# A convolution block followed by a selective scan: another order of work at the scan's first and last units

## The chip, the cores and the metric

The kernel runs on one core of one Trainium2 chip. A core has five engines that run side by side, each through its own list of instructions in order: TensorE (PE), VectorE (DVE), ScalarE (ACT), GpSimd (POOL) and SyncE (SP), which here only issues DMAs. They hand work to each other through semaphores. The metric is the device time of one execution in microseconds (us); the median of three runs of the kernel before is 3618.1 us (3617.41 to 3619.6).

## The reference

Two layers over a batch of 32 images of 96 channels, 56 x 56 pixels, all float32. The first is a ConvNeXt block. The second is a 5x5 depthwise convolution with SiLU, whose result `xs` (32 x 96 x 3136 tokens) goes into a selective scan with N = 4 states per channel. Only the scan is touched by the change:

```
x_dbl = einsum('kd,bdl->bkl', x_proj_w, xs)
dts, Bs, Cs = x_dbl[:, :R], x_dbl[:, R:R+N], x_dbl[:, R+N:]
delta = softplus(einsum('dr,brl->bdl', dt_w, dts) + dt_b)
log_dA = maximum(delta[:, :, None, :] * A, LOG_EPS)
P = exp(cumsum(log_dA, axis=-1))
dB_u = delta[:, :, None, :] * Bs[:, None] * xs[:, :, None]
hs = P * cumsum(dB_u / maximum(P, EPS), axis=-1)
y = einsum('bdnl,bnl->bdl', hs, Cs) + xs * Ds
```

## The kernel before

There are four stages, one after another: the 7x7 convolution, the MLP with its normalisation, the 5x5 convolution, and the scan (from line 587). The first three leave `xs` in DRAM as `conv2_d` (the profile calls it `conv_d`), one row of 32 x 56 values per channel and image row.

The scan works in *steps*. A step `k` is one half (1568 tokens) of one image; 64 steps in all, and two images together make a *piece* of two steps, which is loaded by `load(p)` as one tile `xs_p` of 96 partitions. Each step is cut into three *units* of 32 channels by 4 states, which fill 128 partitions; 192 units. A half step (784 tokens) is numbered `h`.

Per step, in the order in which the data flow:

- `delta_in(k, h)` (L635): matmuls give the input of Softplus in PSUM (`pz`).
- `delta(k, h)` (L643): ACT's Softplus writes it into `du[:, 0]`.
- `delta_x(k, h)` (L649): POOL multiplies it by `xs` into `du[:, 1]`.
- `keep_du(k, h)` (L654): SP stores both to DRAM (`du_d`).
- `rows_bc(k)`, `rows_out(k)` and `spread(k, kind, h)` (L657 to L687): PE and ACT make B (`bt`, kind 0) and C (`ct`, kind 1) on 128 partitions.

Per unit:

- `spread_du(i)` (L689): SP reads `du_d` back with every channel repeated four times, into `rep_i` (two halves of 1568: delta, and delta times x). Five buffers.
- `decay(i)` (L698): three ACT passes over the delta half of `rep_i`; the first is Exp.
- `drive(i)` (L705): POOL multiplies the other half by `bt`.
- `scan(i)` (L709): DVE runs a product scan (L717), a combination with the driven half (L720) and the scan proper (L724), into `hs_i`. The running product lies in PSUM (`pv`).
- `weigh(i)` (L729): POOL saves the last column of the state if another half follows, then multiplies `hs_i` by `ct`.

Per step, at the end: `gather(k, h)` (L737) sums over states and adds `xs * Ds` by matmul into PSUM (`py`), `store(k, h)` (L755) copies it on ACT and ACT issues the DMA to `out`.

The order is written out by hand in the loop at L769 and held by `pin`, which keeps the program's order on each engine. A pass `i` handles unit `i` at its scan; what comes before it is done in passes ahead (`spread_du` four ahead, `decay` two, `drive` one), `weigh` one pass later, `gather` and `store` three or more later. The piece `p` of pass `i` is `(i + 8) // 6`, with `at` the place in it. The first piece is loaded in pass -11; its four Softplus halves are in pass -8, its stores in passes -6 to -3 with the load of the second piece (pass -5) among them, and the first `spread_du` in pass -4. The second piece's Softplus is in pass -2, and `decay(1)` comes after it, in pass -1. All PSUM tiles of the scan but `pv` rotate through two buffers of two banks (`bank_pair`). ACT changes its function table between Softplus and Exp.

## Time and profile before

| What | Value |
|---|---|
| median of three runs | 3618.1 us |
| the profiled execution | 3618.94 us, span 3617.1 us |
| DVE busy / PE / ACT / POOL, share of the span | 74% / 84% / 65% / 55% |
| last store of the 5x5 convolution issued | 1815.13 us |
| first piece's load issued, first matmul on it | 1819.02 us, 1827.04 us |
| first instruction of the first scan (L717) | 1859.70 us |
| first instruction of the second unit's scan | 1875.80 us |
| end of the last unit's scan (L724 at 3599.21 for 3.48) | 3602.69 us |
| end of the span | 3617.1 us |

The profile is one execution; its times count from the start of the span. It has a page with busy shares, the chain that ended last and the costliest groups of instructions. A timeline lists instructions in order of time; a line gives start, duration, engine, line of code, operation, what is written and read, and in brackets how long the engine had been idle and what ended that. "SPq" and "ACTq" are the issues of DMAs, without the transfer itself.

### The profile page before, as it was taken

What the parts mean: (1) busy time and instruction counts of PE and PEld (TensorE: products, weight loads), DVE (VectorE), ACT (ScalarE), POOL (GpSimd) and SP (SyncE); (2) the same over time, 40 slices, a digit from 0 to 9 for tenths busy, and PEclk for the clock granted to TensorE, in tenths of its full rate; (3) what the DMA queues carried; (4) which work ended last, traced back from release to release, by engine and by line L of the source; (5) the groups of instructions that cost most, each with busy time, mean ns of one, the idle gap of its engine ahead of it and who ended that gap; (6) DMA issues with size and microseconds to landing.
All of it is one profiled execution on the core that took longest, in us unless ns stands there. A gap on an engine that the chain in (4) does not pass through costs nothing. (4 is left out here: it accounts for less than half of the span.)

```text
span 3617.1 us, 46656 instructions
## 1 busy us (share of the span) xinstructions
PE 3051.3 (84%) x17290; PEld 1285.1 (36%) x17290; DVE 2659.5 (74%) x1816; ACT 2347.6 (65%) x2166; POOL 1973.9 (55%) x1286
## 2 busy tenths in 40 slices
PE   8999998999999999899848777777777778777775
PEld 5777775333333333333312222222222222222221
DVE  6666666333333333799949999999999999999998
ACT  4555554333333333588758888887888887888884
POOL 2333343222222222000048899998999998999996
PEclk9999999999999999999956667666667666767666
DMA  6655555444444542799977877877877877877873
GB/s 184 194 179 167 172 171 168 157 158 159 157 160 158 158 157 81 220 283 286 276 237 247 279 257 262 286 260 257 282 255 261 288 257 252 287 250 268 286 255 110
DMA packets 307052, 793.92 MB, mean 219 GB/s; under 512 B 124089, under 2 KB 185553, under 8 KB 282153
## 3 DMA queue, kind: packets, MB, share of 16 engines
q1 hardware_dynamic: 260176, 671.66, 57.6%
q0 software_dynamic: 29632, 80.27, 7.1%
q10 hardware_dynamic: 17016, 39.01, 2.9%
q8 instruction: 137, 2.24, 0.3%
q14 instruction: 91, 0.74, 0.1%
HBM read 555.05 MB, written 235.74 MB: 219 GB/s over the span
## 5 line engine op out<-in xcount | busy, mean ns | idle before, releaser
L735 POOL TENSOR_TENSOR hs<-hs,ct 128x1568 f32<-128x1568 f32 x192 | 672.9, 3504 | 106.1 <-DVE hs L724 96.8
L717 DVE TENSOR_TENSOR_SCAN pv<-rep,pv 128x1568 f32<-128x1568 f32 x192 | 664.5, 3461 | 73.3 <-ACT rep L703 56.0
L707 POOL TENSOR_TENSOR rep<-rep,bt 128x1568 f32<-128x1568 f32 x192 | 674.4, 3513 | 15.3 <-DMA rep<-du_d 15.3
L431 ACT ACTIVATE g<-ph,b1p_t 128x896 f32<-128x896 f32 x336 | 320.4, 1005 | 511.6 <-PE ph L421 511.5
L451 DVE SCALAR_TENSOR_TENSOR o<-po,b2r_t,x 128x224 f32<-128x224 f32 x336 | 190.6, 608 | 568.1 <-PE po L440 568.1
L334 PE MATMUL ps<-xq,wt 120*112 120x448 f32 x1536 | 582.9, 540 | 20.2 <-DMA wt<-taps_d 17.9
L463 POOL DMA_DIRECT2D block_d<-o x336 | 183.1, 552 | 659.2 <-DVE o L451 625.2
L334 PEld LDWEIGHTS ps<-xq,wt 120*112 120x112 f32 x1536 | 428.7, 280 | 172.7 <-issue 20.2
L421 PE MATMUL ph<-h,w1r_t 32*128 32x448 f32 x4032 | 438.2, 558 | 24.7 <-DVE h L411 22.6
L652 POOL TENSOR_TENSOR du<-du,xs 96x784 f32<-96x784 f32 x128 | 236.1, 1846 | 372.4 <-ACT du L646 372.4
L638 PE MATMUL pz<-xs,wd_t 96*96 96x392 f32 x512 | 276.5, 705 | 173.2 <-ACT du L646 137.6
L440 PE MATMUL po<-g,w_t 128*32 128x448 f32 x4032 | 413.0, 543 | 0.0
L748 PE MATMUL py<-hs,sel_t 128*32 128x392 f32 x1536 | 328.2, 684 | 72.2 <-POOL hs L735 72.2
L683 PE MATMUL pk<-bn,pick_t 8*128 8x392 f32 x1024 | 288.9, 684 | 100.2 <-ACT y L758 81.2
L720 DVE SCALAR_TENSOR_TENSOR pv<-pv,rep 128x1568 f32<-128x1568 f32 x192 | 345.6, 1800 | 21.1 <-POOL hs L735 1.4
L533 PE MATMUL ps<-xq,wt 128*32 128x448 f32 x3072 | 308.7, 547 | 41.8 <-DMA xq<-block_d 39.8
L724 DVE TENSOR_TENSOR_SCAN hs<-rep,carry_h,pv 128x1568 f32<-128x1568 f32 x96 | 334.0, 3480 | 10.8 <-PE pk L683 0.5
L556 DVE COPY st<-yt 28x896 f32<-28x896 f32 x288 | 317.2, 1101 | 33.0 <-ACT yt L547 14.4
L724 DVE TENSOR_TENSOR_SCAN hs<-rep,pv 128x1568 f32<-128x1568 f32 x96 | 328.4, 3421 | 9.9 <-DVE pv L720 0.5
L701 ACT ACTIVATE rep<-rep,a_t 128x1568 f32<-128x1568 f32 x192 | 308.4, 1606 | 13.5 <-DMA rep<-du_d 13.1
L702 ACT ACTIVATE rep<-rep,lift_t 128x1568 f32<-128x1568 f32 x192 | 307.7, 1602 | 6.2
L703 ACT ACTIVATE rep<-rep,lift_t 128x1568 f32<-128x1568 f32 x192 | 307.6, 1602 | 6.3
(84 smaller groups left out, 3188.3 us busy)
## 6 DMA issues: line engine op xcount, KB each, us to landing
rep<-du_d SPq DMA_DIRECT2D x192, 1568.0 KB
du_d<-du SPq DMA_DIRECT2D x128, 588.0 KB
xq<-block_d SPq DMA_DIRECT2D x192, 225.0 KB
block_d<-o POOLq DMA_DIRECT2D x336, 120.0 KB, 5.8
xt<-in_x_dram SPq DMA_DIRECT2D x192, 196.0 KB
x<-in_x_dram SPq DMA_DIRECT2D x336, 112.0 KB
h<-conv_d SPq DMA_DIRECT2D x84, 448.0 KB
conv_d<-st SPq DMA_DIRECT2D x96, 392.0 KB
```

Source lines behind the costliest of these rows:

```text
L334: nc.tensor.matmul(ps[:, j].rearrange("p (i r) -> p i r", i=BI), lhsT=wv[:KR, t], rhs=xq[:KR, j, :, t : t + W2], start=(t == 0), stop=(t = ...
L421: pin(nc.tensor.matmul(phs[i // 2][:, i % 2, :HALF], lhsT=w1r_t[rows, d, f * 128 : (f + 1) * 128], rhs=hts[n, d][rows, s * HALF : (s + 1) ...
L431: nc.scalar.activation(gt, ph[:, :, :HALF], AF.Gelu, bias=b1p_t[:, f : f + 1], scale=1.0)
L440: pin(nc.tensor.matmul(po[CB * i : CB * i + CB, :HALF], lhsT=w2_t[:, f, CB * d : CB * d + CB], rhs=gts[n, s, f, i // 2][:, i % 2], start=( ...
L533: pin(nc.tensor.matmul(ps[RW * f : RW * f + RW, h, : B * QW].rearrange("p (b q) -> p b q", q=QW), lhsT=wv[:, f, t], rhs=xv[:, :, t : t + Q ...
L556: pin(copy(st[:, :, :, :, f], yt[RW * f : RW * f + QR].rearrange("p h (b q) -> p h b q", q=QW),))
L707: pin(nc.gpsimd.tensor_mul(ut, ut, bts[i // NG]))
L717: pin(nc.vector.tensor_tensor_scan(grown, da, zero, pv[:, last : last + 1] if q else 1.0 / EPS, ALU.mult, ALU.add))
L720: pin(nc.vector.scalar_tensor_tensor(run, in0=grown, scalar=1.0, in1=ut, op0=ALU.min, op1=ALU.mult))
L724: pin(nc.vector.tensor_tensor_scan(ht, da, run, carry_h[:, col : col + 1] if q else 0.0, ALU.mult, ALU.add))
L735: pin(nc.gpsimd.tensor_mul(ht, ht, cts[k]))
L748: pin(nc.tensor.matmul(py[g * DG : (g + 1) * DG, s, :BK], lhsT=sel_t, rhs=hss[k * NG + g][:, cols], start=False, stop=True, tile_position= ...
```

## The change

It touches the first passes and the last of the scan's loop; the passes between keep their order.

At the front, all of the first piece's work is written out in pass -8. The first load is cut into one DMA per image. A one-column Softplus (`warm`) is put ahead of everything. For the first image, delta alone is stored and read back (`spread_du(0, deltas)`), and delta times x, on DVE, follows with a store and a read of its own. Units 1 and 2 are read next, then the second piece is loaded, then `decay(0)`, `drive(0)`, and the second image's delta, on POOL as before. In pass -2 `decay` and `drive` of units 1 and 2 stand ahead of the second piece's Softplus. At the end, the last `weigh` is cut in two (DVE and POOL), the last step's `gather` takes units 0 and 1 in the pass before unit 2's, and the last `store` is copied by DVE and issued by SP.

```diff
         def load(p):
...
-            pin(nc.sync.dma_start(
-                xt, conv2_d[:, q * HQ : (q + 1) * HQ, b * W : (b + NI) * W]
-            ))
+            rows = conv2_d[:, q * HQ : (q + 1) * HQ, b * W : (b + NI) * W]
+            for i in range(1 if p else NI):
+                cols = slice(None) if p else slice(i * W, (i + 1) * W)
+                pin(nc.sync.dma_start(xt[:, :, cols], rows[:, :, cols]))
...
-        def delta_x(k, h):
+        def delta_x(k, h, engine=nc.gpsimd):
...
-            pin(nc.gpsimd.tensor_mul(u, d, tokens(k, h, 2)))
+            pin(engine.tensor_mul(u, d, tokens(k, h, 2)))
...
-        def keep_du(k, h):
-            pin(nc.sync.dma_start(du_d[k][:, :, h * HT : (h + 1) * HT], dus.pop((k, h))))
+        def keep_du(k, h, part=slice(0, 2)):
+            pin(nc.sync.dma_start(
+                du_d[k][:, part, h * HT : (h + 1) * HT], dus[k, h][:, part]
+            ))
...
-        def spread_du(i):
+        def spread_du(i, part=slice(0, 2)):
...
+            to = reps[i][:, part].rearrange("p i t -> p (i t)")
+            du = du_d[k, g * DG : (g + 1) * DG, part, :]
+            src = bass.AP(du.tensor, du.offset, [du.ap[0], [0, N], [1, to.shape[1]]])
+            pin(nc.sync.dma_start(to, src))
...
-            pin(nc.gpsimd.tensor_mul(ht, ht, cts[k]))
+            if i < units - 1:
+                pin(nc.gpsimd.tensor_mul(ht, ht, cts[k]))
+            else:
+                for engine, cols in (nc.vector, slice(0, HT)), (nc.gpsimd, slice(HT, CH)):
+                    pin(engine.tensor_mul(ht[:, cols], ht[:, cols], cts[k][:, cols]))
...
-        def gather(k, h):
+        def gather(k, h, parts=range(NG)):
...
-        def store(k, h):
+        def store(k, h, copy=nc.scalar.copy, queue=nc.scalar):
...
+            if p == 0 and at == 0:
+                deltas, products = slice(0, 1), slice(1, 2)
+                warm = pool.tile([C, 1], F32, name="warm", bufs=1)
+                pin(nc.scalar.activation(warm, dtb_t, AF.Softplus))
+                for h in range(2):
+                    delta_in(0, h)
+                for h in range(2):
+                    delta(0, h)
+                for h in range(2):
+                    keep_du(0, h, deltas)
+                spread_du(0, deltas)
+                for h in range(2):
+                    delta_x(0, h, nc.vector)
+                    keep_du(0, h, products)
+                rows_bc(0)
+                rows_out(0)
+                spread_du(0, products)
+                for u in range(1, NG):
+                    spread_du(u)
+                load(1)
+                for h in range(2):
+                    spread(0, 0, h)
+                decay(0)
+                drive(0)
+                for h in range(2):
+                    delta_in(1, h)
+                    delta(1, h)
+                    delta_x(1, h)
+                    keep_du(1, h)
+                continue
...
+            ready = {-2: [1, 2], -1: [], 0: []}.get(i, [i + 2])
+            driven = {-2: [1, 2], -1: [], 0: [], 1: []}.get(i, [i + 1])
...
-            at_unit(i + 2, decay)
-            at_unit(i + 1, drive)
+            for u in ready:
+                if u:
+                    at_unit(u, decay)
+            for u in driven:
+                if u:
+                    at_unit(u, drive)
...
-            if g == 0 and 0 <= after < steps:
+            if g == 0 and 0 <= after < steps - 1:
                 gather(after, 0)
                 store(after, 0)
                 gather(after, 1)
+            if i == units - 1:
+                for h in range(2):
+                    gather(steps - 1, h, range(NG - 1))
+            if i == units:
+                for h in range(2):
+                    gather(steps - 1, h, range(NG - 1, NG))
+                store(steps - 1, 0)
+                store(steps - 1, 1, nc.vector.tensor_copy, nc.sync)
```

## The prediction

> **What bounds the kernel now.** I read the page first, then the timelines of DVE, ACT, POOL and SP from 1795 to 1960 us, then the last 80 us. Between its two ends the scan is DVE's: from the second unit at 1875.80 to 3602.69 it runs 191 units, 9.04 us each, and its three rows alone give 3.461 + 1.800 + about 3.45 = 8.71.
>
> ```profile
> L717 DVE TENSOR_TENSOR_SCAN pv<-rep,pv 128x1568 f32<-128x1568 f32 x192 | 664.5, 3461 | 73.3 <-ACT rep L703 56.0
> L720 DVE SCALAR_TENSOR_TENSOR pv<-pv,rep 128x1568 f32<-128x1568 f32 x192 | 345.6, 1800 | 21.1 <-POOL hs L735 1.4
> ```
>
> Of the 73.3 us that DVE stood idle before L717, 44.63 + 7.31 are the start and 1.15 follows at unit 7. So the time is: when DVE gets going, plus the units, plus the 14.4 us after DVE's last scan. The change works on the first and the last term. DVE's start:
>
> ```profile
> 1859.70 3.43 DVE L717 TENSOR_TENSOR_SCAN pv<-rep,pv 128x1568 f32<-128x1568 f32 x1 [44.63 <-ACT rep L703]
> 1875.80 3.43 DVE L717 TENSOR_TENSOR_SCAN pv<-rep,pv 128x1568 f32<-128x1568 f32 x1 [7.31 <-ACT rep L703]
> 1893.57 3.43 DVE L717 TENSOR_TENSOR_SCAN pv<-rep,pv 128x1568 f32<-128x1568 f32 x1
> 1930.41 3.49 DVE L717 TENSOR_TENSOR_SCAN pv<-rep,pv 128x1568 f32<-128x1568 f32 x1 [1.15 <-ACT rep L703]
> ```
>
> These are units 0, 1, 3 and 7. What they waited for stands on SP's queue:
>
> ```profile
> 1819.02 0.31 SPq L621 DMA_DIRECT2D xs<-conv_d  x1
> 1834.17 0.65 SPq L655 DMA_DIRECT2D du_d<-du  x1
> 1834.86 0.61 SPq L621 DMA_DIRECT2D xs<-conv_d  x1
> 1835.99 5.43 SPq L655 DMA_DIRECT2D du_d<-du  x1
> 1846.95 0.55 SPq L695 DMA_DIRECT2D rep<-du_d  x1
> ```
>
> The second store of the first image stands behind the second piece's load, and the read of unit 0 waits 5.5 us more for it. Unit 1 was in place by 1863.77 (POOL drives it then), but its decay starts at 1870.90, because ACT does the second piece's Softplus from 1859.68 to 1869. The end:
>
> ```profile
> 3602.84 3.48 POOL L735 TENSOR_TENSOR hs<-hs,ct 128x1568 f32<-128x1568 f32 x1 [5.59 <-DVE hs L724]
> 3606.37 2.82 PE L748 MATMUL py<-hs,sel_t 128*32 128x392 f32 x8 [7.56 <-POOL hs L735]
> 3609.13 2.02 PE L741 MATMUL py<-xs,dsm_t 96*96 96x392 f32 x4
> 3611.07 1.52 PE L748 MATMUL py<-hs,sel_t 128*32 128x392 f32 x12
> 3612.64 0.81 ACT L758 COPY y<-py 96x784 f32<-96x784 f32 x1 [2.60 <-PE py L748]
> 3613.48 0.32 ACTq L759 DMA_DIRECT2D out_dram<-y  x1
> ```
>
> The transfer takes from 3613.48 to the end at 3617.1, 3.6 us for 294 KB.
>
> **What the Trainium skill says.** "ScalarE: Activation LUTs", What ACT_TABLE_LOAD costs, gives about 1.28 us for a change of table; the trace has 1.28 at 1830.01, after the wait for PE. "DMA: Bandwidth & Descriptors", Why small descriptors are slow, gives three cycles on top of one per 32 bytes: 17 for 448 bytes, 10 for 224; no row here shows 224. "SBUF — State Buffer", Who interferes with whom, says that a DVE instruction with two SBUF inputs and a GpSimd one that reads SBUF exclude each other; the scan's DVE rows have one operand in PSUM, so the trace doesn't test it. "TensorE: Matmul & The Clock Gate", Part 1, says that the clock doubles after some 3.4 us of work; here matmuls on `pz` take 0.65 us from 1827.04 and 0.33 from about 1832.3.
>
> **The front, step by step.**
> *Load.* The first piece took 8.0 us from issue to matmul, about 5.2 of them transfer (DMA is busy from 1821 to about 1826). Half of it in as many pieces of half the size takes between 2.6 and 5.2 us; by the skill's 10/17 it is 3.1. I take 1.6 us earlier, 1825.4, with 0 and 2.6 as ends. I assume that the matmul waits for its own image alone: ACT wrote its column of the last `st` (1809.05) before DVE wrote the interleaved others (1812.22), so interleaved parts are told apart.
> *Delta.* The first Softplus comes 2.97 us after the data, as before, without the table load (`warm` does it while ACT waits, 19.20 us idle). The second half's matmuls end 5.3 us after the data; 0.91 for Softplus: 1831.9.
> *Store and read delta.* The store is as large as the final output's, 3.6 us: 1835.5. The read of a full unit took 7.85 us (1846.95 to Exp at 1854.80); half the bytes at 430 GB/s (windows 1855 to 1870) save 1.9, and no store shares the queue: 5.2, so 1840.7. Decay is three passes of 1.64: 1845.6, first scan instruction, 14 us earlier than before.
> *Products.* DVE's multiplication, about 0.95 from 1.083 for 128x896 in the normalisation, lies under the wait for the store. Its two stores are issued after the read of delta, for SP waits at that read; with 1.9 us of read and 2.5 of store (602 KB at 236 GB/s, window 1837 to 1841) ahead they land at about 1843. Read 5.2, `drive` 3.5: L720 at 1851.7, unit 0 ends at 1857.1.
> *Units 1 and 2, second piece.* From 1843 the queue holds 0.8 + 1.6 + 1.6 MB of reads, 9.3 us at 430 GB/s, then the second piece, 5.2. With 1.9 to start and 1.2 to finish, unit 1 is there at 1851.7, unit 2 at 1855.5, the second piece at 1860.6; before it was there at 1845.57. Decays end at 1857.2 and 1862.1 and scans run 1857.3 to 1866.2 and 1866.2 to 1875.1. Image 1's products on POOL stand behind `drive(0)` and end at 1855.4; their stores follow the load, about 1867, and unit 3's read is there by 1873.
> *The new wait.* In pass -2 PE's matmuls on the second piece wait for it to 1860.6, and behind them on PE stand `ct` of step 0, `rows_bc(1)` and `bt` of step 1; behind these on ACT stands `decay(3)`. From the load: 3.0 to the first Softplus; with two banks, the four are done after 11.9 if PE stays at 0.65, after 9.3 if it speeds up; two copies of `ct` 2.1, `pn` and its copy 2.9, `bt` 3.8, table 1.3, decay 4.9, which makes 26.9 or 23.5 with the faster matmuls counted throughout. Unit 3 can scan at 1884.1 to 1887.5, against 1893.57: 6 to 9.5 earlier, though DVE stands idle for 9 to 12 us before it.
> *What is late next.* POOL can weigh unit 0 only with `ct`, 11 to 14 us after the load. Three weighs, one `drive`, two products (3 x 3.5 + 3.5 + 2 x 1.85) bring `weigh(2)` to 1889.6 to 1892.4, against 1897.46. It releases `gather`, the two copies at 1900.38 and 1906.07, after which ACT runs `bt`, `decay(6)`, Softplus and `decay(7)` without slack: the wait of 1.15 at unit 7. So what arrives at unit 7 is 5.1 to 7.9. I take 6.5. Beyond it the order is the old one, and before only 2.9 us of idle time before L717 remain to the end.
>
> **The end.** After 3602.69 DVE weighs half a tile (0.95), POOL the other (1.75). The gather of units 0 and 1 and of `xs` is done by then, hidden beside unit 191's scan. What remains are eight matmul records of one column group, which can't run beside each other (four of a group take 1.52 us fast, 2.8 slow): 5.4 slow, about 4.3 if the clock rises midway, as it did at 3610. From 3603.8 to 3608.1 or 3609.2; DVE's copy from PSUM is about 0.97 (0.55 for 384 columns in `w1r_t`), the output 3.6: 3612.7 to 3613.8, so 3.3 to 4.4 less. If DVE and POOL exclude each other, 0.9 to 1.7 of it is lost. I take 3.8.
>
> **Sum.** 6.5 + 3.8 = 10.3 us off the profiled execution's 3618.94, or 3608.6; the median of runs lies 0.8 lower: 3608.
>
> **Rivals.**
> *Everything is hidden.* Should ACT reach `decay(3)` by 1875 after all, DVE runs on from unit 2: 18.5 + 3.8, 3596. For it: DVE's own units leave no more. Against it: PE's and ACT's order put eight dependent exchanges behind the second piece. Chance 0.10.
> *The gain at the front is given back.* The second piece comes 6.5 us later than I have it, or the first image's matmul waits for both halves in pieces that cost as much as whole ones (5.2 + 1.6 later): then the change doesn't do what it says at the front, and the end alone remains, 3614. For it: the load has been put behind 4 MB of reads, and the queue did hold SP up (5.43 us for one issue). Against it: 430 GB/s while such reads ran. Chance 0.20.
> *The second piece becomes the bound.* If the reads of units 0 to 2 ran at 215 GB/s (window 1875 to 1880 has that) and the load with them at half speed, the load would land about 14 us later; PE, and ACT and POOL behind it, stand still. From 10.3 us late on the whole is a loss, from 17.5 on over 0.2%; at 19 late, 3627. Against it: little else moves then. Chance 0.08.
>
> **How the numbers follow.** The forecast has 0.62, with 3603 to 3611 as its own range. A measurement of this kernel can tell about 0.2%, 7.2 us, from no change: below 3610.9 is faster, above 3625.3 slower. Faster: nearly all of the forecast and the first rival, 0.70. Within 0.2%: the second, a little of the forecast and of the third, 0.22. Slower 0.08. The range, 3601 to 3616, leaves out most of the first and third rivals.
>
> **What would show it.** First L717 near 1846, L720 of unit 0 some 2.5 us after the first scan's end; `pz` of the second piece starting near 1860; DVE idle for 9 to 12 us before unit 3, released by ACT L703; unit 7 at about 1924. At the end, 10 to 11 us after the last scan instead of 14.4. It would be wrong if unit 3 starts later than 1891, or if the middle's 9.04 us per unit changes.

## The result, and the profile after

| What | Before | After |
|---|---|---|
| median of the timed runs | 3618.42 us (3612.85 to 3621.63, 6 runs) | 3598.3 us (3597.0 to 3600.45, 6 runs) |
| ratio to before, 95% interval | | 0.9946 [0.9933, 0.9959] |
| the profiled execution, its span | 3618.94 us, 3617.1 us | 3600.45 us, 3598.7 us |

The changed kernel is faster by 20.1 us by the medians and by 18.4 us between the two spans, where 10.3 had been forecast. The kernel after ran again in two later sets, beside the kernel before on the same chip: 3596.47 us against 3614.91 (18.4 less) and 3598.98 against 3615.83 (16.9 less).

An absolute time of the trace holds everything that came before it. The first piece's load is issued at 1819.02 us in the trace before and at 1817.32 in the one after. The program up to there is the same, and over all traces of this study the issue lies between 1809.96 and 1819.02 without relation to any edit. So from here on the landmarks count **from the issue of the first piece's load**:

| From the issue of the first load, us | Before | After | Change |
|---|---|---|---|
| first matmul on the first piece | 8.02 | 5.32 | -2.70 |
| first scan, unit 0 | 40.68 | 24.78 | -15.90 |
| first matmul on the second piece | 26.55 | 39.82 | +13.27 |
| scan of unit 3 | 74.55 | 61.95 | -12.60 |
| scan of unit 7 | 111.39 | 98.51 | -12.88 |
| end of the last scan | 1783.67 | 1771.09 | -12.58 |
| from there to the end of the span | 14.41 | 10.29 | -4.12 |

So, between these two traces, 12.6 come from the front and 4.1 from the end, and 1.7 of the difference of the spans lie before the change begins. From unit 7 to the last scan's end it is 1672.3 before and 1672.6 after: the middle is as it was, as far as single traces tell, which differ by up to 6 us there (see below). From the load's issue to the end of the span the kernel after, traced three times, is 16.7 to 18.1 us shorter than the one trace of before.

The two rows of the costliest groups that answer to those shown of before (columns: line, engine, operation, operands, count | busy, mean ns of one | idle time before):

```profile
L721 DVE TENSOR_TENSOR_SCAN pv<-rep,pv 128x1568 f32<-128x1568 f32 x192 | 664.5, 3461 | 42.8 <-ACT rep L707 24.9
L724 DVE SCALAR_TENSOR_TENSOR pv<-pv,rep 128x1568 f32<-128x1568 f32 x192 | 345.6, 1800 | 22.6 <-POOL rep L711 1.6
```

Read alone, the first row tells too much: 73.3 - 42.8 is 30.5 us less idle time. But DVE now has work earlier, and part of its idle time stands before that. From DVE's timeline of the kernel after, the two products and the first rows of units 0, 1, 3 and 7:

```profile
1826.52 0.97 DVE L653 TENSOR_TENSOR du<-du,xs 96x784 f32<-96x784 f32 x1 [12.94 <-ACT du L647]
1828.88 0.97 DVE L653 TENSOR_TENSOR du<-du,xs 96x784 f32<-96x784 f32 x1 [1.40 <-ACT du L647]
1842.10 3.43 DVE L721 TENSOR_TENSOR_SCAN pv<-rep,pv 128x1568 f32<-128x1568 f32 x1 [12.24 <-ACT rep L707]
1847.15 1.80 DVE L724 SCALAR_TENSOR_TENSOR pv<-pv,rep 128x1568 f32<-128x1568 f32 x1 [1.63 <-POOL rep L711]
...
1852.50 3.43 DVE L721 TENSOR_TENSOR_SCAN pv<-rep,pv 128x1568 f32<-128x1568 f32 x1
...
1879.27 3.43 DVE L721 TENSOR_TENSOR_SCAN pv<-rep,pv 128x1568 f32<-128x1568 f32 x1 [9.10 <-ACT rep L707]
...
1915.83 3.49 DVE L721 TENSOR_TENSOR_SCAN pv<-rep,pv 128x1568 f32<-128x1568 f32 x1 [0.87 <-ACT rep L707]
```

The products take 12.94 + 0.97 + 1.40 + 0.97 = 16.3 us out of the first scan's idle time, and L724 has 1.5 more; 30.5 - 16.3 - 1.5 = 12.7, which is the front's gain. Unit 1 follows unit 0 without a pause (7.31 before), and the new pause of 9.10 stands at unit 3. SP's queue in the kernel after:

```profile
1817.32 2.30 SPq L624 DMA_DIRECT2D xs<-conv_d  x2
1826.51 2.68 SPq L656 DMA_DIRECT2D du_d<-du  x2
1831.49 0.52 SPq L700 DMA_DIRECT2D rep<-du_d  x1
1832.06 1.06 SPq L656 DMA_DIRECT2D du_d<-du  x2
1838.73 1.81 SPq L700 DMA_DIRECT2D rep<-du_d  x3
1840.59 0.60 SPq L624 DMA_DIRECT2D xs<-conv_d  x1
```

The read of unit 0's delta goes out at 14.2 us after the load instead of 27.9, and the second piece's load (1840.59) behind all reads. What unit 3 waits for is ACT's and PE's round on the second piece. From ACT's timeline of the kernel after, from the second piece's first Softplus to the decay of unit 3, and then the copies of the first outputs:

```profile
1860.07 0.91 ACT L647 ACTIVATE du<-pz,dtb_t 96x784 f32<-96x784 f32 x1 [2.04 <-PE pz L639]
1862.26 0.91 ACT L647 ACTIVATE du<-pz,dtb_t 96x784 f32<-96x784 f32 x1 [1.27 <-PE pz L639]
...
1868.35 0.81 ACT L674 COPY bn<-pn 128x784 f32<-128x784 f32 x1 [0.66 <-PE pn L665]
1870.94 0.81 ACT L690 COPY bt<-pk 128x784 f32<-128x784 f32 x1 [1.78 <-PE pk L686]
...
1874.37 1.60 ACT L705 ACTIVATE rep<-rep,a_t 128x1568 f32<-128x1568 f32 x1
...
1892.00 0.81 ACT L767 COPY y<-py 96x784 f32<-96x784 f32 x1 [0.41 <-PE py L758]
```

And the end of the kernel after, from the timeline of all engines:

```profile
3588.44 0.97 DVE L743 TENSOR_TENSOR hs<-hs,ct 128x784 f32<-128x784 f32 x1
3588.55 2.57 POOL L743 TENSOR_TENSOR hs<-hs,ct 128x784 f32<-128x784 f32 x1 [5.59 <-DVE hs L728]
...
3588.63 5.00 PE L758 MATMUL py<-hs,sel_t 128*32 128x392 f32 x16
...
3593.72 0.97 DVE L767 COPY y<-py 96x784 f32<-96x784 f32 x1 [4.30 <-PE py L758]
3594.72 0.34 SPq L768 DMA_DIRECT2D out_dram<-y  x1
```

POOL's half is 2.57 long although half of 3.50 is 1.75. DVE's half ends at 3589.41, and POOL's 1.71 us after that: the two did not run beside each other. PE's sixteen records (each matmul of the kernel leaves two in the trace) are eight of units 0 and 1 for the second output, which PE had not come to before, and eight of unit 2; they end 2.5 us after POOL does. The last output takes from 3594.72 to the end of the span at 3598.7, and the way from the last scan (3588.41) to the end is 10.29.

### The profile page after: what moved, and what is told of

Read it like the earlier page. It is cut to its first block, busy times and chain, and to the rows that moved or that the text cites. A ratio compares the mean times of both kernels' runs of the same rounds, so it can differ in the third digit from the quotient of the medians.

```text
span 3598.7 us, 46673 instructions
## 1 busy us (share of the span) xinstructions
PE 3053.6 (85%) x17290; PEld 1288.2 (36%) x17290; DVE 2666.7 (74%) x1820; ACT 2352.2 (65%) x2168; POOL 1969.5 (55%) x1284
## 5 line engine op out<-in xcount | busy, mean ns | idle before, releaser
L721 DVE TENSOR_TENSOR_SCAN pv<-rep,pv 128x1568 f32<-128x1568 f32 x192 | 664.5, 3461 | 42.8 <-ACT rep L707 24.9
L724 DVE SCALAR_TENSOR_TENSOR pv<-pv,rep 128x1568 f32<-128x1568 f32 x192 | 345.6, 1800 | 22.6 <-POOL rep L711 1.6
L728 DVE TENSOR_TENSOR_SCAN hs<-rep,pv 128x1568 f32<-128x1568 f32 x96 | 328.4, 3420 | 10.3 <-PE pz L639 0.5
L750 PE MATMUL py<-xs,dsm_t 96*96 96x392 f32 x512 | 304.8, 737 | 10.9 <-ACT bn L674 5.4
```

The source lines that it names most:

```text
L721: pin(nc.vector.tensor_tensor_scan(grown, da, zero, pv[:, last : last + 1] if q else 1.0 / EPS, ALU.mult, ALU.add))
L724: pin(nc.vector.scalar_tensor_tensor(run, in0=grown, scalar=1.0, in1=ut, op0=ALU.min, op1=ALU.mult))
L728: pin(nc.vector.tensor_tensor_scan(ht, da, run, carry_h[:, col : col + 1] if q else 0.0, ALU.mult, ALU.add))
```

## The experiments

Each kernel is the one after with the edit that is named. Landmarks are from the issue of the first load, as above, and "end" is the way from the last scan's end to the end of the span. The kernel after itself, three times, sets the scatter of one trace:

| Kernel | Second piece | Unit 3 | Unit 7 | Last scan's end | End |
|---|---|---|---|---|---|
| after | 39.82 | 61.95 | 98.51 | 1771.09 | 10.29 |
| e8_after_again | 40.12 | 62.79 | 99.69 | 1770.69 | 9.34 |
| e16_after_third | 39.45 | 61.40 | 97.85 | 1771.77 | 9.30 |

No edit; the first was expected to do this:

> The changed kernel, unaltered, to stand beside the others on the same chip. 15 to 20 us below the kernel before; in its trace unit 3 again about 62 us and unit 7 about 98.5 us after the first load's issue, the last scan's end about 1771 us after it, and 10.3 us from there to the end of the span. If these stretches differ by 2 us or more from the first trace of the changed kernel, the differences of 1 to 3 us seen between single traces tell nothing.

and the second this:

> The changed kernel, unaltered, beside the other two: 16 to 20 us below the kernel before, unit 3 at 62 to 62.8 and unit 7 at 98.5 to 99.7 us after the first load's issue.

They gave 3596.47 us, 0.9952 [0.9939, 0.9964], and 3598.98 us, 0.9954 [0.9941, 0.9966]. A landmark up to unit 7 is good to about 1 us in most traces. The arrival of the first image strays further: with the load cut, the first matmul comes 5.2 to 5.4 us after the issue in thirteen traces, but 6.65 in e11_last_weigh_whole and 7.17 in e3_delta_with_product, whose edits don't touch the load. From unit 7 on, traces of all kernels differ by up to 6 us (1667.8 to 1674.2 to the last scan's end), so the early landmarks tell small things apart that the times can't. The kernel before has one trace.

### What each part is worth

**The first load in one piece (e2_one_load).**

```diff
-            for i in range(1 if p else NI):
-                cols = slice(None) if p else slice(i * W, (i + 1) * W)
-                pin(nc.sync.dma_start(xt[:, :, cols], rows[:, :, cols]))
+            pin(nc.sync.dma_start(xt, rows))
```

> The first piece is one DMA again. Theory (the second piece sets unit 3, and everything up to it follows the first image's arrival one for one): first matmul 8.0 instead of 5.3 us after the issue, the second piece 2.7 us later, unit 3 at about 64.6 us after the first load's issue instead of 62.0, time 2.7 us above the changed kernel, about 3601. Rival (the load's size is hidden by the waits on the queue behind it): the first matmul 2.7 later, but unit 3 within 1 us of 62.0.

Measured: 3602.48 us, 0.9965 [0.9952, 0.9977]. The first matmul comes 8.16 us after the load instead of 5.3, unit 3 at 65.65 instead of 61.4 to 62.8, the last scan's end at 1775.21 instead of 1770.7 to 1771.8. PE's timelines of the kernel after and of this one:

```profile
1822.64 5.26 PE L639 MATMUL pz<-xs,wd_t 96*96 96x392 f32 x8 [16.72 <-DMA xs<-conv_d]
```

```profile
1824.63 4.75 PE L637 MATMUL pz<-xs,wd_t 96*96 96x392 f32 x8 [18.81 <-DMA xs<-conv_d]
```

1822.64 - 1817.32 is 5.32; here 1824.63 - 1816.47 is 8.16. So cutting the load is worth 2.8 us at the start, and it reaches the second piece (42.75 instead of 39.5 to 40.1) and unit 3: the chain from the first image to unit 3 has no slack. At unit 3 it looks like more than 2.8, but there PE's sixteen records on the second piece took 8.84 us, 0.6 to 1.3 more than in the three traces of the kernel after.

**The end undone (e1_end_undone), and the whole last `weigh` alone (e11_last_weigh_whole).** The first has the old end in all three edits; the second has this edit alone:

```diff
-            if i < units - 1:
-                pin(nc.gpsimd.tensor_mul(ht, ht, cts[k]))
-            else:
-                for engine, cols in (nc.vector, slice(0, HT)), (nc.gpsimd, slice(HT, CH)):
-                    pin(engine.tensor_mul(ht[:, cols], ht[:, cols], cts[k][:, cols]))
+            pin(nc.gpsimd.tensor_mul(ht, ht, cts[k]))
```

> The end of the scan is as before (last weigh whole on POOL, last gather and stores in the old passes), the front as changed. If front and end add up and don't touch, the stretch from the last scan's end to the end of the span goes back from 10.3 to 14.4 us, unit 3 starts 62 us after the first load's issue as in the changed kernel, and the time is 4.1 us above it, about 3602.4. If the two ends are not independent (a rival: the last step's work in the old order also holds up the last units), DVE's last scan comes later too and it is more than 5 us.

> The last weigh is whole on POOL again, all else as changed. Theory (the half on DVE lets the first gather start 2.5 us earlier, and that is a good part of what the end gains): POOL takes 3.5 instead of 2.6 us, the gather of the last unit starts 3.5 instead of 1.0 us after the last scan, and the stretch from the last scan's end to the end of the span is 12 to 13 us instead of 9.3 to 10.3; time 2 to 3 us above the changed kernel. Rival (PE's slow matmuls from 1 to 5 us after the scan hide it): the stretch stays below 11.

Measured: e1 3606.29 us, 0.9974 [0.9965, 0.9983], its end 16.79 us long; e11 3599.62 us, 0.9957 [0.9945, 0.997], its end 11.54, between what its theory and its rival gave. The timeline of e1's end:

```profile
3581.95 3.48 POOL L739 TENSOR_TENSOR hs<-hs,ct 128x1568 f32<-128x1568 f32 x1 [5.58 <-DVE hs L728]
...
3585.49 2.82 PE L754 MATMUL py<-hs,sel_t 128*32 128x392 f32 x8 [7.55 <-POOL hs L739]
...
3588.24 2.93 PE L746 MATMUL py<-xs,dsm_t 96*96 96x392 f32 x4
...
3591.10 2.84 PE L754 MATMUL py<-hs,sel_t 128*32 128x392 f32 x12
```

The same three PE groups stand in the kernel before with 2.82, 2.02 and 1.52. The profile also gives the clock that PE was granted, as a share of the full clock; in the stretches looked at it is 0.50 or 1.00, or a mean of the two. A stretch of before and one of e1, with from and to, length, busy time (and instructions) of PE, its weight loads, DVE, ACT and POOL, then the granted clock, the DMA share and GB/s:

```profile
3610.00:3614.00 4.00, 2.59 (x16) 0.71 (x14) 0.00 (x0) 0.85 (x2) 0.00 (x0) 0.99 0.26 75
```

```profile
3590.00:3594.00 4.00, 3.93 (x14) 0.58 (x12) 0.00 (x0) 0.01 (x1) 0.00 (x0) 0.50 0.26 77
```

In the kernel before the clock rose midway, in e1 it stayed at half up to the last matmul. That makes 2.2 of the 2.4 us between the two ends. So the end's edits are worth 4.1 us against the trace of before and 6.5 to 7.5 against e1's. The times agree with the larger figure: e1's ratio is 0.0020 to 0.0028 above those of the kernel after, some 7 to 10 us, with 3 us to either side in each interval. They give the front less than the landmarks do: e1, with the new front and the old end, is 9.4 us below the kernel before by its ratio, and its interval goes from 6.1 to 12.7. Up to unit 3 and unit 7 e1's own trace agrees with the kernel after (61.34 and 97.64).

Of the end's gain the cut `weigh` is 2.2 us, if e11 is set against the two traces of the kernel after in which the clock had come up in time as well (9.30 and 9.34), and 1.2 against the first (10.29). In e11 PE ran its last eight records in 2.82:

```profile
3590.51 3.49 POOL L739 TENSOR_TENSOR hs<-hs,ct 128x1568 f32<-128x1568 f32 x1 [5.59 <-DVE hs L728]
...
3594.05 2.82 PE L754 MATMUL py<-hs,sel_t 128*32 128x392 f32 x8 [2.71 <-POOL hs L739]
```

In the kernel after POOL's cut row ends 0.92 earlier than this whole one would (2.57 instead of 3.49; some 0.8 are lost while DVE works). The other 1.3 come from PE: the first output's records need only DVE's half and run while POOL is still at the other, so that four records in 1.50 are left at the end (e8_after_again) instead of eight in 2.82. What else the end gains must come from the gather of units 0 and 1, and of `xs`, which no longer stands behind POOL; no run has this alone. It isn't the last store on DVE and SP: from PE's last matmul to the end of the span it is 4.5 and 4.7 us in before and in e1, and 4.6 to 5.1 in the fifteen traces with the new store (DVE's copy takes 0.97, ACT's 0.81).

**Without `warm` (e13_no_warm).**

```diff
-                warm = pool.tile([C, 1], F32, name="warm", bufs=1)
-                pin(nc.scalar.activation(warm, dtb_t, AF.Softplus))
```

> Without the one-column Softplus ahead of the first piece. The table load of 1.28 us then stands between the first image's matmul and its Softplus. Theory: first scan 1.3 us later (26.1 instead of 24.8 to 24.9 us after the first load's issue), the second piece about 1.3 later, unit 3 at about 63.5, time 1.3 us above the changed kernel. Rival (the waits on the queue take it up): unit 0 later, unit 3 not.

Measured: 3594.4 us, 0.9944 [0.993, 0.9957]; first scan at 25.11 instead of 24.2 to 24.9, unit 3 at 62.45. ACT's timeline of this kernel:

```profile
1821.57 1.28 ACT L647 ACT_TABLE_LOAD   x1 [15.58 <-PE pz L639]
1822.86 0.91 ACT L647 ACTIVATE du<-pz,dtb_t 96x784 f32<-96x784 f32 x1
1824.14 0.91 ACT L647 ACTIVATE du<-pz,dtb_t 96x784 f32<-96x784 f32 x1 [0.38 <-PE pz L639]
```

The table load is back, but the second Softplus still waits 0.38 for PE (1.45 in the kernel after): 1.07 of the 1.28 fall into time in which ACT would have waited for PE anyway. The 1.3 us that were expected did not come: `warm` is worth at most some 0.3 us here, which is within the scatter of the landmarks. (Where the prediction takes 1.28 us for a change of table from the Trainium skill, "ScalarE: Activation LUTs", What ACT_TABLE_LOAD costs, that section has a drain of 1.38 us besides. Only the load shows here: in the kernel after an Exp chain ends at 1842.06, and Softplus starts at 1843.38.)

### What holds unit 3

**Delta and delta times x together, as before (e3_delta_with_product).**

```diff
                 for h in range(2):
-                    keep_du(0, h, deltas)
-                spread_du(0, deltas)
-                for h in range(2):
                     delta_x(0, h, nc.vector)
-                    keep_du(0, h, products)
+                    keep_du(0, h)
                 rows_bc(0)
                 rows_out(0)
-                spread_du(0, products)
-                for u in range(1, NG):
+                for u in range(NG):
                     spread_du(u)
```

> The first image's delta and product are stored together and read together (two stores and one read instead of four and two); the product stays on DVE, all else as changed. Theory (the second piece sets unit 3): the first scan starts about 4 us later, but the queue has two round trips less, the second piece lands about 3 us earlier, and unit 3 with it: time 3 us below the changed kernel, about 3595. Rival (it is the early start of unit 0 that pays): unit 3 and the time 4 us later, about 3602.

Measured: 3597.6 us, 0.9954 [0.9942, 0.9967], no different from the kernel after by its times. The trace is of the slowest of the five executions (3601.86, 3.7 above the next), and its first matmul comes 1.85 later after the load than in the kernel after, so not all of its delay is the edit's. In it unit 0 scans at 30.41 (5.6 later), the second piece is there at 39.30, and unit 3 scans at 68.84 instead of 62, where 3 us earlier had been expected. ACT's timeline of this kernel, then PE's of this one and of the kernel after:

```profile
1839.85 1.60 ACT L705 ACTIVATE rep<-rep,a_t 128x1568 f32<-128x1568 f32 x1 [7.11 <-DMA rep<-du_d]
...
1857.08 1.60 ACT L707 ACTIVATE rep<-rep,lift_t 128x1568 f32<-128x1568 f32 x1
1858.70 1.28 ACT L647 ACT_TABLE_LOAD   x1
1860.00 1.71 ACT L647 ACTIVATE du<-pz,dtb_t 96x784 f32<-96x784 f32 x2
1863.97 0.91 ACT L647 ACTIVATE du<-pz,dtb_t 96x784 f32<-96x784 f32 x1 [2.27 <-issue]
```

```profile
1853.64 5.51 PE L639 MATMUL pz<-xs,wd_t 96*96 96x392 f32 x8 [20.00 <-DMA xs<-conv_d]
1860.96 5.54 PE L639 MATMUL pz<-xs,wd_t 96*96 96x392 f32 x8 [1.80 <-ACT du L647]
```

```profile
1857.14 7.72 PE L639 MATMUL pz<-xs,wd_t 96*96 96x392 f32 x16 [19.12 <-DMA xs<-conv_d]
```

The first decay waits 7.11 us for the whole of unit 0's read; decays 1 and 2 and the Softplus of image 1 follow without a pause and keep ACT busy to 1858.70. The second piece's matmuls began at 1853.64, but Softplus can begin only at 1860.00, and PE, which has two buffers, stops in the middle. Its two groups of eight then take 5.51 and 5.54 us, where the sixteen without a pause take 7.72 in the kernel after. From the first Softplus to unit 3 it is 23.2 us instead of 19.2. PE's granted clock is 0.50 over all of this stretch; in the kernel after it is 1.00 from 1861.65 to 1868.48.

**The second piece's load ahead of units 1 and 2 (e6_load_first).**

```diff
+                load(1)
                 for u in range(1, NG):
                     spread_du(u)
-                load(1)
```

> The second piece is loaded ahead of units 1 and 2's reads, all else as changed. If the second piece's arrival alone sets unit 3, it lands 7 us earlier and so do unit 3 and the time (about 55 us after the first load's issue). If ACT's chain sets it, with the decays of units 1 and 2 ahead of Softplus (shown by the run with delta and its product together, where the piece came 2.4 us earlier and unit 3 didn't), units 1 and 2 come 5 us later, their decays end 5 us later, Softplus begins about 3 us later, and unit 3 and the time are 2 to 4 us later than in the changed kernel.

Measured: 3605.3 us, 0.9973 [0.9964, 0.9983], 8.8 us above the kernel after in the same set. The second piece comes 7 us earlier (32.96), and unit 3 is 8.5 us later (70.43), where 2 to 4 had been expected. ACT's timeline of this kernel:

```profile
1852.52 1.60 ACT L705 ACTIVATE rep<-rep,a_t 128x1568 f32<-128x1568 f32 x1 [7.09 <-DMA rep<-du_d]
...
1863.46 1.71 ACT L647 ACTIVATE du<-pz,dtb_t 96x784 f32<-96x784 f32 x2
```

Now unit 1's read stands behind the load, its decay waits 7.09, and Softplus starts at 47.25 instead of 42.75. PE stops again between two groups of eight (5.27 and 5.54), its clock, which had come up at 1854.07, is back at half from 1857.48 on, and the chain to unit 3 takes 23.2 again. In the kernel after ACT is free for Softplus at 1858.03 and the first result is there at 1860.07: **the two chains into the second piece's Softplus are equal to 2 us.** Moving ACT's chain forward alone brings nothing, moving the piece forward alone brings 2 us at most, and moving either at the other's cost loses.

**Softplus of the second piece ahead of decays 1 and 2 (e5_softplus_first).** In pass -2 the loop over `ready` and `driven` stands behind the one over the four halves:

```diff
-            for u in ready:
-                if u:
-                    at_unit(u, decay)
-            for u in driven:
-                if u:
-                    at_unit(u, drive)
+            def ahead():
+                for u in ready:
+                    if u:
+                        at_unit(u, decay)
+                for u in driven:
+                    if u:
+                        at_unit(u, drive)
+
+            if i != -2:
+                ahead()
...
                     delta(p * NI + j, h)
+            if i == -2:
+                ahead()
```

> In pass -2 the second piece's Softplus stands ahead of the decay and drive of units 1 and 2 again, all else as changed. Theory (ACT is the chain of the front: what it waits for in order holds everything behind): ACT waits for the second piece with unit 1's data there, unit 1 starts about 54 us after the first load's issue instead of 35, unit 3 about 72 instead of 62, time 9 to 10 us above the changed kernel. Rival (the second piece's arrival alone sets unit 3): unit 1 later, but unit 3 within 3 us of 62 and the time within 3 us.

Measured: 3608.19 us, 0.9983 [0.9976, 0.9989], 11.7 above the kernel after in the same set. DVE's timeline of this kernel has unit 1 at

```profile
1867.15 3.43 DVE L721 TENSOR_TENSOR_SCAN pv<-rep,pv 128x1568 f32<-128x1568 f32 x1 [19.43 <-ACT rep L707]
```

and unit 3 at 71.94, 10 later than in the kernel after: as the theory said, ACT stands at a Softplus for 14.97 us, and decays 1 and 2 behind it. With the load this late, the order of the decays is the part of the change that must go with it.

**B of step 1 made early (e4_bt_ahead).** `bt` of step 1 is made with that of step 0, in pass -8, and `ct` of step 0 behind decays 1 and 2, so that less stands between the second piece's Softplus and `decay(3)`; the later passes leave both out:

```diff
-                rows_bc(0)
-                rows_out(0)
+                for k in range(2):
+                    rows_bc(k)
+                    rows_out(k)
...
-                for h in range(2):
-                    spread(0, 0, h)
+                for k in range(2):
+                    for h in range(2):
+                        spread(k, 0, h)
...
+            if i == -2:
+                for h in range(2):
+                    spread(0, 1, h)
```

> The second step's B (rows and both copies) is made in the first pass, while ACT and PE wait for unit 0, and the first step's C right behind the decay of unit 2; so of the work between the second piece's arrival and the decay of unit 3 only Softplus is left. Theory (unit 3 waits for the order of ACT and PE behind the second piece, not for its data): unit 3 starts 4 to 7 us earlier than 62.0 after the first load's issue, time 4 to 6 us below the changed kernel, about 3593. Rival (unit 3 waits for its own data, read after the second image's stores): unit 3 within 1 us of 62.0.

Measured: 3595.41 us, 0.9947 [0.9934, 0.9961]. Unit 3 comes at 54.88, 7 us earlier, as expected, but unit 7 at 98.14 as before. A line of ACT's timeline, then one of DVE's, of this kernel:

```profile
1882.84 1.60 ACT L705 ACTIVATE rep<-rep,a_t 128x1568 f32<-128x1568 f32 x1 [5.54 <-DMA rep<-du_d]
```

```profile
1913.72 3.49 DVE L721 TENSOR_TENSOR_SCAN pv<-rep,pv 128x1568 f32<-128x1568 f32 x1 [5.28 <-ACT rep L707]
```

Unit 5's decay now waits 5.54 for its read, and unit 7 waits 5.28 for ACT. What was won at unit 3 is lost again before unit 7, and the 4 to 6 us that were expected of the time did not come.

### What is late next

**The third piece's load later, on top of that (e9_bt_ahead_third_later).** The third piece's load was ahead of unit 5's read on the queue:

```diff
-            if at == 3 and p + 1 < PC and (p + 1) != 1:
+            if at == 3 and p + 1 < PC and (p + 1) not in (1, 2):
                 load(p + 1)
             if i + AHEAD >= NG:
                 at_unit(i + AHEAD, spread_du)
+            if i == 1:
+                load(2)
```

> The kernel with the second step's B made ahead, and the third piece's load put behind the read of unit 5 instead of ahead of it. In the former, decay of unit 5 waited 5.54 us for its data, and of the 7 us gained at unit 3 only 0.4 were left at unit 7. If that wait is what gave them back, decay of unit 5 doesn't wait, unit 7 starts at 93 to 95 us after the first load's issue instead of 98, and the time is 3 to 5 us below the changed kernel. If not (rival: the second Softplus round and POOL's weighs hold unit 7, whatever the data), unit 7 stays within 1.5 us of 98.

Measured: 3595.84 us, 0.9949 [0.9936, 0.9962]. The wait of unit 5's decay is gone, unit 7 comes at 96.94, 0.9 to 2.8 earlier than in the three traces of the kernel after, where 93 to 95 had been expected. ACT's timeline of this kernel:

```profile
1878.81 0.81 ACT L767 COPY y<-py 96x784 f32<-96x784 f32 x1 [1.35 <-PE py L758]
...
1882.66 0.81 ACT L767 COPY y<-py 96x784 f32<-96x784 f32 x1 [3.04 <-PE py L758]
```

These are the two output copies that the prediction named as late next; in the kernel after they wait at most 0.41, here 1.35 and 3.04.

**The first `weigh` early, on top of that (e15_first_weigh_early).**

```diff
             if i == -2:
                 for h in range(2):
                     spread(0, 1, h)
+                scan(0)
+                weigh(0)
...
-            at_unit(i - 1, weigh)
+            if i != 1:
+                at_unit(i - 1, weigh)
...
-            at_unit(i, scan)
+            if i:
+                at_unit(i, scan)
```

> The kernel with the second step's B made ahead and the third piece's load behind unit 5's read, where the scan of unit 0 and its weigh are also written out in pass -2, so that on POOL the weigh stands ahead of the second piece's products. Theory (unit 7 is held by weigh, gather and the two copies ahead of the decay of unit 6): POOL's third weigh ends 3 to 5 us earlier, ACT's waits of 1.35 and 3.04 before these copies shrink to under 1 together, and unit 7 starts at 92.5 to 94.5 us after the first load's issue instead of 96.9; the last scan's end comes 5 us or more ahead of the changed kernel's (1771 after the load's issue, give or take 3). Rival (ACT's own work from unit 3 on): unit 7 stays above 96.

Measured: 3596.78 us, 0.9947 [0.9933, 0.9961]. The copies wait 0.41 again, but unit 7 is not earlier (98.95), nor is the last scan's end 5 us ahead (1769.92): ACT's timeline of this kernel has

```profile
1890.10 1.60 ACT L705 ACTIVATE rep<-rep,a_t 128x1568 f32<-128x1568 f32 x1 [3.10 <-DMA rep<-du_d]
```

which is unit 6's decay, waiting for its read. Each of these three kernels removes one wait and meets another: a read, the copies, a read. None can be told from the kernel after by its time.

**PE kept busy (e10_pe_kept_busy, e14_pe_kept_busy_14, e12_bt_ahead_pe_kept_busy).** Matmuls whose result nobody reads are put at the end of pass -8, 24 of them, then 14, and 20 on top of e9, to have PE's clock up when the second piece comes:

```diff
+                fill = bank_pair("fill")
+                for _ in range(24):
+                    pin(nc.tensor.matmul(
+                        half(fill[:C], 0), lhsT=wd_t, rhs=tokens(0, 0, 4),
+                        start=True, stop=True,
+                    ))
                 continue
```

> The changed kernel with 24 more matmuls behind the second image's, into a PSUM tile that nothing reads; they fill most of the 19 us in which PE waits for the second piece. The output is not touched. Theory (PE's clock is a term of the wait for unit 3: matmuls on a piece take 0.65 us after a pause and 0.33 in work): the four Softplus of the second piece end 2.5 to 3.5 us earlier after its arrival, unit 3 starts 59 to 60 us after the first load's issue instead of 62 to 62.8, time 2 to 3 us below the changed kernel, near 3594. Rival (ACT's own passes set the pace from the second piece on): unit 3 within 1 us of 62.

> The changed kernel with 14 filler matmuls (28 records) into a tile that nothing reads; they begin about 26.6 us after the first load's issue, when a PSUM pair comes free, and should end before the second piece is there at 39.8 to 40.1. Theory (PE's clock is a term): the sixteen records on the second piece take 5.4 us as in the run with 24 fillers instead of 7.7 to 8.3, and unit 3 starts 2 us earlier, 60 to 60.7 us after the first load's issue; time 1 to 2 us below the changed kernel beside it. Rival (ACT sets the pace): unit 3 within 0.7 us of 62.

> The kernel with the second step's B made ahead and the third piece's load behind unit 5's read, with 20 more matmuls into a tile that nothing reads, in PE's wait ahead of the second piece. Theory: Softplus of the second piece is paced by PE at the slow clock there too, so unit 3 starts at about 53.5 instead of 55.9 us after the first load's issue; unit 7, held by the two copies after the first gather, gains 1 us or less on 96.9; time 0 to 1 us below that kernel's 3595.8. If unit 7 gains as much as unit 3 (rival), the time is 2 to 3 us below.

Measured: e10 3602.23 us, 0.9963 [0.9951, 0.9976], unit 3 at 66.33; e14 3597.39 us, 0.9948 [0.9936, 0.9961], unit 3 at 61.74; e12 3602.33 us, 0.9963 [0.9951, 0.9976], unit 3 at 58.71 against 55.89 in e9. PE's timelines of e10 and of e14:

```profile
1842.29 19.43 PE L815 MATMUL fill<-xs,wd_t 96*96 96x392 f32 x48 [9.21 <-ACT du L647]
1861.56 5.43 PE L639 MATMUL pz<-xs,wd_t 96*96 96x392 f32 x16
```

```profile
1843.12 11.91 PE L815 MATMUL fill<-xs,wd_t 96*96 96x392 f32 x28 [4.64 <-ACT du L647]
1856.55 7.17 PE L639 MATMUL pz<-xs,wd_t 96*96 96x392 f32 x16 [1.52 <-DMA xs<-conv_d]
```

With 24 the fillers end 6 us after the piece is there (by the 39.8 of the kernel after); the sixteen records then take 5.43 instead of 7.72, at the full clock, but start late. With 14 they end 1.52 before it, and the records take 7.17: the granted clock is still 1.00 in the pause, falls to 0.50 at 1858.34, when PE has been at the records for 1.8 us, and is back at 1.00 from 1861.75 on. From the second piece to unit 3 it is 20.47 in e10 (counted from the late start), 21.14 in e14 and 21.9 to 22.7 in the kernel after. So the full clock is worth 1.5 to 2.2 us between the second piece and unit 3 by e10, and it can't be had for sure this way: neither run brings unit 3 to the 59 to 60.7 that were expected, and e14's 61.74 is within what its rival gave. In e12 the fillers also stood ahead of `ct` on PE and were a plain delay.

## Why the prediction was wrong in its size

The forecast was 3608, with 3601 to 3616 as the range; the time is 3598.3. The direction and the places were right, and **the term of the front was mis-sized: 6.5 us taken, 12.6 measured** between the two traces. Half of the 6.1 between them lies in the new wait before unit 3, put down with 23.5 to 26.9 us and measured with 22.1; 1.8 lie in the way to the second piece, and the rest in a loss between unit 3 and unit 7 that did not come. By the prediction's own steps, counted from the load:

| Step of the prediction | Predicted | Measured | Off by |
|---|---|---|---|
| first image there | 6.4 | 5.3 | 1.1 |
| first scan | 26.6 | 24.8 | 1.8 |
| second piece there | 41.6 | 39.8 | 1.8 |
| second piece to unit 3 | 23.5 to 26.9 | 22.1 | 3.1 from the middle |
| gain at unit 3 | 6 to 9.5 | 12.6 | 4.8 from the middle |
| gain at unit 7 | 5.1 to 7.9, 6.5 taken | 12.9 | 6.4 |
| gain at the end | 3.8 | 4.1 (6.5 to 7.5 against e1) | 0.3 (2.7 to 3.7) |

*Load.* "I take 1.6 us earlier", with 2.6 as the upper end. It was 2.70, and e2_one_load shows 2.8 as the load's own share. The reading under it was short: the trace before has its DMA engines busy for the whole load from about 1819.9 to 1826.1, 6.2 us and not 5.2. The estimate by the Trainium skill, "DMA: Bandwidth & Descriptors", Why small descriptors are slow, 10/17 of the whole for the half, was 3.1 us of the 5.2; of 6.2 it is 3.6, an estimate too, and saves 2.6. The price itself shows in the time that packets took, the DMA share times the stretch: 6.6 us before and 7.7 after for both halves, 1.17 as much, where the page's figures give 20/17 or 1.18. But the packets overlap, and both halves together were through in about 6.3 us (1818.2 to 1824.5), hardly more than the whole. In most traces the matmul waits for its own image alone, as was assumed.

*Store and read.* "3.6 us" for the store of delta was borrowed from the final output. (The sum ahead of it is 0.3 high: 1825.4 + 5.3 + 0.91 is 1831.6 and not 1831.9.) The last Softplus ends at 1828.85, and the read that waits for the store is issued at 1831.49: 2.6. The read to Exp takes 5.71 instead of 5.2. The first scan is 1.8 earlier than forecast, 1.1 of it by the load. The second piece comes 1.8 earlier likewise; e3 and e6 show that this alone is no gain unless ACT is free as well, and in the kernel after it is, by 2 us.

*The new wait.* This is the step that failed most: its sum was too long, not its order. DVE does stand idle before unit 3, 9.10 us (forecast 9 to 12), released by ACT, and the order of the exchanges is the one written down. But "3.0 to the first Softplus" was 2.93, and the rest was 19.2 us where 20.5 to 23.9 had been added up: the four Softplus were done 8.7 us after the piece (11.9 or 9.3 forecast), and `pn` with its copy took 1.5 (2.9 forecast). The middle of a slow and a fast PE was taken. ACT was free and took each result at once, so PE got all sixteen records without a pause, and its clock rose on the way. The slow case exists: 23.2 in e3 and e6, where PE pauses and the granted clock is 0.50 from the first Softplus to unit 3. Of the 4.0 us more than 19.2, 1.7 lie in the four Softplus, 0.9 in the two copies of `ct` and 1.3 in `pn` and its copy, each of them behind matmuls that ran at half the clock; `bt` and the decay take as long as in the kernel after.

*What is late next.* "I take 6.5" kept the chain from `weigh` over `gather` to the copies as a loss of 1.3 between unit 3 and unit 7. It was none, 0.3 were won. `weigh(2)` ends at 1885.84, and the second copy starts 6.2 later at 1892.00, after 0.41 of waiting; in the kernel before it was 1897.46 to 1906.07, 8.6, with 4.89 of waiting, and PE's clock was at half there throughout. The mechanism is real: e9 brings unit 3 some 6 us forward, and the copies wait 1.35 and 3.04.

*The end.* 3.3 to 4.4 less was forecast and 4.1 found between the two profiles. The named risk, that DVE and POOL exclude each other, came true at its lower bound: some 0.8 us, with POOL's half ending 1.71 after DVE's. The Trainium skill, "SBUF — State Buffer", Who interferes with whom, says so for such a pair, and the trace agrees. "Done by then" was not quite so for the gather of units 0 and 1: with PE at half its clock the second half begins at 3588.63, after the last scan. Where the clock comes up in time the new end is 9.3 (the other two traces). The old end was read from one trace, in which the clock rose; it is 14.4 to 16.8, the new one 9.3 to 10.3, and so the term is 4.1 to 7.5, of which the forecast saw only the lower part. Which of these an execution gets is luck, as far as these traces show: the order of work is the same.

*The rivals.* "Everything is hidden" had 3596 and came nearest in number, but not by its mechanism: DVE does not run on from unit 2, and its 9.10 us before unit 3 are there. The gain at the front was not given back, and the second piece became no bound that costs more than before. The middle's 9.04 us per unit did not change between the two traces.

*The range.* Nearly every term of the front was taken from its cautious side, and they were not independent: a load that is early, and a PE that isn't interrupted, shorten each step behind them. 4.9 of the 6.1 us lie up to unit 3 by the table above. The range's lower end of 3601 left no room for all of them going well at once.

*What stays open.* The landmarks give 16.7 us (12.6 + 4.1); the three comparisons of times gave 20.1, 18.4 and 16.9. The remainder of 0 to 3 us could be the end, if runs of the kernel before mostly have its slow form, as the ratio of e1 suggests; it is also of the size by which the issue of the first load and the stretch behind unit 7 vary between traces. How the sum falls to its two parts is open by as much: landmarks give the front 12.6 and the end 4.1 to 7.5, the times of e1 some 9.4 (6.1 to 12.7) and 7 to 10. No kernel with the old front and the new end was run.

## What to carry to other kernels

Count landmarks from the first instruction that the change touches, not from the span's start, and set the idle time of a row beside that of the rows that now stand in front of it. Where a stall is fed by two chains (here ACT's own decays and the second piece's way through PE), write down when each is free: the slack between them, 2 us here, is the most that moving the later one can bring, and e6 shows that a move at the other's cost loses several. Where a chain's length depends on whether an engine is kept going, forecast its two lengths as two cases by what feeds it, and don't take the middle.

## What the hardware showed that was not expected

- PE's granted clock changes only on a grid of 3.413 us. In the kernel after it rises at 1827.52, 1837.76 and 1861.65 and falls at 1830.93, 1841.17 and 1868.48, all whole multiples of 3.413 apart (to 0.01 us), and the same holds for all changes between 1817 and 1913 us in each of the seventeen traces. Where PE's work falls on this grid differs from trace to trace: on the second piece the clock rose 3.7 us after PE's start in e1 and 4.5 in the kernel after, with the fillers of e10 6.9 after their start; and the sixteen records of the second piece, begun at half the clock and run without a pause, took 7.29 (e1) to 8.91 us (e15). The Trainium skill, "TensorE: Matmul & The Clock Gate", Part 1, has the clock double after some 3.4 us of work; these traces show 3.7 to 6.9.
- A short pause was enough to be followed by a lower clock, and not at once. After 11.9 us of matmuls and a pause of 1.52 us (e14) it fell 1.8 us into the next records and stayed at half for one step of the grid, 3.41 us: sixteen records took 7.17 us, against 5.43 at the full clock and 7.72 after 19 us of rest, of which 4.5 were at half.
- The same three groups of matmuls at the kernel's end took 2.82 + 2.02 + 1.52 = 6.4 us in one trace and 2.82 + 2.93 + 2.84 = 8.6 in another with the same order of work there (before, and e1), as the clock rose midway or not.
- Halving the pieces of a strided load from 448 to 224 bytes raised the time that its packets took from 6.6 to 7.7 us for the same bytes, but the load was through in 6.3 us instead of 6.2. With the first half on its own DMA, its first use came 5.3 us after the issue instead of 8.0 to 8.2.
